# Graph transformer layer followed by a graph attention layer: where the scores stand among TensorE's products, and how one bias row is made

## The chip, the cores and the metric

The kernel runs on one core of one Trainium2 chip, in one launch. The metric is the device time of that core in microseconds (us). Everything is float32.

## The reference, cut to what matters

x has 128 batches of 128 tokens with 512 features, adj 128 matrices of 128 x 128. Two layers follow one another, each on a layer norm with a relu:

```python
h = relu(layernorm(x))
q, k, v = h @ Wq.T + bq, h @ Wk.T + bk, h @ Wv.T + bv     # 8 heads of 64
scores = (q @ k.T) / 8 * (adj + adj)                      # per head
ctx = softmax(scores) @ v
x = x + ctx @ Wo.T + bo

h = relu(layernorm(x))
Wh = h @ W
e = leaky_relu(Wh @ a[:512] + (Wh @ a[512:]).T)
att = softmax(where(adj > 0.5, e, -9e15), axis=1)
x = x + elu(att @ Wh)
```

## The kernel before, in words

**Tiling.** A step p handles a pair of batches, called a and b (64 steps). A group g is two steps, four batches. In layer 0 the projections of a whole group are made by a scheme of 26 block products in place of 32 (a fast matrix multiplication in blocks): for each of the 26 terms n, `Qn` (`product_qk`, L297) makes the products for q and k, and `Vn` (`product_v`, L306) that for v. Their left or right factors are blocks of the normalised input (`hA`) or sums of such blocks, made by `Tn` on GpSimd (`make_form`, L282, tile `tf`, 8 buffers). Four chains of running sums in PSUM, for q/k and for v, are read by `An` (`take_qk`) and `Bn` (`take_v`).

**A step of layer 0.** `sca` and `scb` (`scores`, L367) make the scores of batch a and of batch b. Each head has 64 features, so one product contracts over 64 partitions only, and two heads stand in the two halves of the array's rows. The scores of one batch fill two PSUM tiles of a bank each. `ata0/1` and `atb0/1` (`weigh`, L374, VectorE) read them; maxima, exponentials, sums and division follow (`mx`, `ex`, `rc`, `nm`), then a transposition in blocks with a trip through DRAM (`fl`, `bl`, `pl`). `pca` and `pcb` (`context`, L435) make the contexts: 64 output columns per head, two heads in the two halves of the array's columns. `pe` (ScalarE) and `cs0` to `cs3` (VectorE) read them. `o0` to `o6` (`product_rows`, L346) are the seven products of the output projection, added to x by `od...`.

**A step of layer 1.** `st`, `pw`, `nm`, `h2`, `d..` make the norm and the two dot products, `wm` to `sw` the attention weights, `g0`, `g1` (`gather1`, L528) gather, `ge` and `gs0` to `gs3` read, `w0` to `w6` (`product_rows` again) are seven products, read by `zc...` (ScalarE, L542) and `wd...` (VectorE).

**Banks.** All PSUM tiles come from one pool of 8 banks (`ps1`). A `row_a` tile has two halves: products 0, 2, 4, 5 run up a sum in the first half, which is read after each of them, and product 1 ("b") has the second half. Products 3 and 6 have a tile of their own, `row_c`.

**Order.** Nothing is scheduled by the compiler: three lists, `HEAD`, `ORDER` and `TAIL`, written out in the kernel, give the order of all steps. `ORDER` is run 27 times, for the groups 2 to 28, once for each; a word such as `scb:0` names a step and its distance in p. Each engine takes its own instructions in this order. In `ORDER` before, the steps of TensorE around scores and contexts stand thus: `V23 pca:1 pcb:1 scb:0 w2`, `o6 sca:-1 V5`, `V12 pca:0 pcb:0 scb:-1 Q17` and `o3 sca:-2 Q24`.

**The bias row.** The weights of attention sum to 1, so the bias of v can be added behind the output projection: c = Wo bv + bo - 1. It is made once, in `HEAD`: `ccp` (`product_c`, L578) multiplies 16 blocks of Wo with columns of bv, one output column each; `ccd` (L584) adds bo and -1; `ccs` (`turn_column`, L600) turns the four columns into rows on all partitions with four transposes; `cch` (L603) copies them to `c_sb`. `sh` (GpSimd, L270) adds `c_sb` to x.

Of the kernel before, what the change touches and what calls it, by code (L numbers as in the profile page):

```python
# [13 lines left out]
P = 128  # L14
# [3 lines left out]
H = 8  # L18
# [6 lines left out]
def kernel(  # L25
# [113 lines left out]
    bo_sb = column(bo, "bo")  # L139
# [110 lines left out]
    def fetch0(p):  # L250
        r = rows0[p]
        rows0[p] = small.tile([P, 2 * S, 2], F32, name="mr", bufs=2)
        nc.sync.dma_start(
            rows0[p].rearrange("p k s -> p (k s)"), r.rearrange("b p s -> (b p s)").partition_broadcast(P)
        )
# [21 lines left out]
    def make_form(g, k):  # L277

        a, op, b = FORMS[k]
        forms[g, 2 * C + k] = grp.tile([P, 2 * S], F32, name="tf", bufs=8)  # L280
        eng = nc.gpsimd
        eng.tensor_tensor(forms[g, 2 * C + k], form(g, a), form(g, b), OP.add if op == "+" else OP.subtract)  # L282
# [55 lines left out]
    def product_rows(p, left, w, which, n):  # L338

        la, wb, bank = PRODUCTS[n]  # L340
        own = "c" if bank == "c" else "a"
        if n == 0 or n == 3:
            accs[p, which, own] = ps1.tile([P, 2, E // 2], F32, name="row_" + own, tag="ps1")
        acc = row_acc(p, which, bank)
        for c in range(2):
            nc.tensor.matmul(  # L346
                acc, left[:, la, c, :], w[:, wb, c, :], start=n in (0, 3) and c == 0, stop=c == 1, skip_group_check=True
            )

    def row_acc(p, which, bank):  # L350
        return accs[p, which, "c" if bank == "c" else "a"][:, 1 if bank == "b" else 0, :]
# [18 lines left out]
    def weigh(b, k):  # L370
        p, i = divmod(b, 2)
        if b not in ats:
            ats[b] = work.tile([P, H, S], F32, name="at"), *(small.tile([P, H], F32, name=n) for n in ("nmx", "sums", "rs"))
# [196 lines left out]
    ucol, ccol = const.tile([P, 2, C], F32, name="ucol"), const.tile([P, 1, C], F32, name="ccol")  # L570


    def product_c():
        onces["pm"] = pm = ps1.tile([P, C], F32, name="pm", tag="ps1")
        for j in range(C):
            ms = slice(j % 2 * P, (j % 2 + 1) * P)
            for c in range(C):
                nc.tensor.matmul(  # L578
                    pm[:, j : j + 1], wo_sb[:, 2 * (c // 2) + j // 2, c % 2, ms], bv_sb[:, c : c + 1],
                    start=(c == 0), stop=(c == C - 1),  # L580
                )

    def sum_c():
        nc.vector.scalar_tensor_tensor(ccol[:, 0, :], onces["pm"], -1.0, bo_sb, op0=OP.add, op1=OP.add)  # L584
# [17 lines left out]
    def keep_row(name, dst):  # L602
        nc.scalar.copy(dst, onces[name].rearrange("p c k -> p (c k)"))  # L603
# [16 lines left out]
    def listed(text, mark):  # L620
# [3 lines left out]
        lx@0 t0@-5 lx@1 t0@-4 t1@-4 pp@1 L3@0 t1@-5 W0@0 L0@0 hn0@1 tp0@1 ev0@1 hn1@1 tp1@1 W2@0 pp@0 Lo1@0 ev1@1  # L624
        T4@-2 W13@0 hn1@0 tp1@0 ev1@0 hn0@0 tp0@0 T0@-2 Q0@-2 ev0@0 T5@-2 T1@-2 T2@-2 T3@-2 T6@-2 lx@2 t0@-3 W1@0
        la@0 l0@-2 t0@-2 t1@-2 W3@0 Q1@-2 A1@-2 t1@-3 pp@2 L1@0 W4@0 V1@-2 B1@-2 A0@-2 W7@0 W5@0 W8@0 hn1@2 Q3@-2
        A3@-2 Q5@-2 W9@0 hn0@2 V0@-2 B0@-2 W6@0 Q2@-2 A2@-2 tp1@2 ev1@2 W14@0 Q7@-2 L2@0 W16@0 W11@0 W10@0 Q4@-2
        A4@-2 V3@-2 W25@0 V2@-2 B2@-2 W12@0 Q6@-2 W19@0 W15@0 B3@-2 V5@-2 V7@-2 pp@3 hn1@3 V4@-2 B4@-2 tp1@3 W21@0
        V6@-2 hn0@3 tp0@3 ev0@3 tp0@2 T8@-2 W17@0 B7@-2 W18@0 W29@0 T7@-2 T9@-2 T10@-2 T11@-2 T12@-2 A7@-2 V13@-2
        Q13@-2 W20@0 V9@-2 Q9@-2 W26@0 W28@0 B13@-2 B6@-2 A6@-2 Q8@-2 W27@0 W24@0 W33@0 l0@-1 Lo0@0 Lw0@0 la@-1 W31@0  # L630
        W22@0 t0@-1 t1@-1 A13@-2 W23@0 W30@0 V8@-2 V15@-2 A9@-2 Q11@-2 A8@-2 B8@-2 B9@-2 V11@-2 V10@-2 ev1@3 Q15@-2
        A15@-2 B11@-2 A11@-2 Q10@-2 Lu@0 B15@-2 B10@-2 Q17@-2 T0@0 s0@-1 A17@-2 A10@-2 V12@-2 B12@-2 T13@-2 Q14@-2
        V17@-2 B17@-2 A14@-2 T16@-2 T14@-2 V14@-2 Q12@-2 ev0@2 T7@0 T4@0 T1@0 A12@-2 B14@-2 l0@0 t0@0 V19@-2 Q19@-2
        V16@-2 Q16@-2 A19@-2 Q21@-2 B16@-2 Q0@0 B19@-2 V21@-2 V18@-2 A16@-2 Q18@-2 t1@0 A21@-2 sca@0 Lw1@0 cu00@0
        Q20@-2 B21@-2 ata0@0 ata1@0 T15@-2 s0@0 V23@-2 A20@-2 mxa@0 T2@0 V20@-2 V1@0 B1@0 A0@0 T5@0 B20@-2 W32@0
        exa3@0 exa1@0 exa0@0 Q22@-2 A22@-2 Q23@-2 V22@-2 B22@-2 A23@-2 W34@0 rca0@0 Q24@-2 A24@-2 B23@-2 exa2@0
        nma0@0 rca1@0 nma2@0 V24@-2 B24@-2 l0@1 t0@1 t1@1 Wo0@0 V0@0 nma1@0 nma3@0 fla@0 B0@0 scb@0 T8@0 Q25@-2
        V25@-2 T3@0 V3@0 B3@0 atb0@0 Q1@0 A1@0 V2@0 Q2@0 B2@0 V4@0 B4@0 atb1@0 T9@0 T6@0 T15@0 B25@-2 Q3@0 V6@0 A2@0
        Q4@0 T10@0 A3@0 Q5@0 Q7@0 V5@0 V7@0 B6@0 V8@0 mxb@0 exb3@0 A25@-2 Wo1@0 cu01@0 sca@1 scb@1 l0@2 t1@2 exb1@0
        exb0@0 rcb0@0 exb2@0 A7@0 rcb1@0 f0@1 B8@0 V10@0 t0@2 Ww0@0 lT@1 hd0@1 nmb1@0 A4@0 Q6@0 Q9@0 hd1@1 B7@0 V9@0  # L640
        nmb2@0 nmb0@0 nmb3@0 flb@0 ata1@1 ata0@1 A6@0 Q8@0 Ww1@0 A9@0 B9@0 V11@0 Q11@0 s0@1 T11@0 T12@0 mxa@1 Q13@0
        A13@0 B10@0 A8@0 Q10@0 V13@0 Q15@0 B13@0 V15@0 bla@0 pla@0 pca@0 exa2@1 A10@0 A11@0 B15@0 exa3@1 rca1@1 Q12@0
        exa1@1 exa0@1 A15@0 Q17@0 f0@0 lT@0 T13@0 T0@2 V14@0 rca0@1 B11@0 Ww3@0 nma3@1 A12@0 Wo3@0 V12@0 B12@0 nma0@1
        nma1@1 nma2@1 fla@1 A17@0 atb1@1 Q14@0 T14@0 l0@3 blb@0 plb@0 la@1 atb0@1 B14@0 V17@0 B17@0 ccp@0 ccd@0 A14@0
        mxb@1 pcb@0 T16@0 pea@0 peb@0 ccs@0 Q19@0 o0@0 t0@3 Wo2@0 A19@0 V19@0 B19@0 exb0@1 Q16@0 exb2@1 V16@0 o1@0
        exb3@1 cs2@0 cs0@0 A16@0 V0@2 V21@0 cs1@0 hd0@0 hd1@0 cch@0 Q18@0 Q20@0 exb1@1 rcb0@1 sh@0 B21@0 nmb1@1
        nmb0@1 Q21@0 A20@0 Q22@0 T7@2 f0@2 B16@0 V18@0 rcb1@1 cs3@0 od0@0 o2@0 bla@1 A21@0 sca@2 A22@0 sh@1 Q23@0
        V20@0 V23@0 Q24@0 nmb3@1 nmb2@1 pla@1 flb@1 ata1@2 ata0@2 T1@2 od2@0 o4@0 t1@3 mxa@2 exa1@2 o3@0 T3@2 od1@0
        od4@0 sup0@0 B20@0 V22@0 exa0@2 o5@0 A23@0 B22@0 V24@0 rca0@2 A24@0 Q25@0 od4c@0 o6@0 exa3@2 nma1@2 od5@0
        B24@0 blb@1 plb@1 V25@0 st0@0 exa2@2 rca1@2 od6@0 B23@0 lt@0 nma0@2 sua0@0 T2@2 T4@2 sh@2 T8@2 nma3@2 nma2@2  # L650
        s0@2 T5@2 Q1@2 A1@2 Q0@2 A25@0 st1@0 A0@2 pw@0 cu10@0 nm@0 B25@0 cu11@0 pca@1 lT@2 hd0@2 lT@3 h20@0 d00@0
        pcb@1 peb@1 h21@0 d10@0 scb@2 cs0@1 fla@2 Q3@2 pea@1 V1@2 B1@2 px@0 f0@3 atb0@2 pd@0 bla@2 atb1@2 Q2@2 cs2@1
        B0@2 V2@2 V3@2 B2@2 V4@2 o0@1 o1@1 A2@2 Q4@2 B3@2 V5@2 V7@2 A3@2 mxb@2 B4@2 od0@1 cs1@1 hd1@2 o2@1 od2@1 B7@2
        la@2 hd0@3 hd1@3 sup1@0 o3@1 A4@2 exb1@2 exb3@2 V9@2 exb0@2 sua1@0 B9@2 exb2@2 d11@0 o4@1 od4@1 Q5@2 Q6@2
        A6@2 cs3@1 o5@1 od4c@1 o6@1 pv@0 d01@0 wm@0 od1@1 rcb1@2 od5@1 rcb0@2 pr@0 m1@0 od6@1 st0@1 st1@1 s0@3 e1@0
        sw@0 nmb2@2 V6@2 sca@3 Q7@2 Q8@2 l0@4 g1@0 g0@0 t1@4 A7@2 Q9@2 nmb3@2 nmb1@2 B6@2 nmb0@2 flb@2 pla@2 blb@2
        pw@1 nm@1 T9@2 T6@2 ata1@3 ata0@3 ge1@0 A8@2 Q10@2 ge0@0 T10@2 T11@2 T12@2 A9@2 V11@2 Q11@2 B11@2 gs0@0 A10@2
        mxa@3 h20@1 V8@2 w0@0 h21@1 B8@2 V10@2 Q13@2 gs2@0 gs1@0 A11@2 exa2@3 exa1@3 T16@2 T13@2 V13@2 w1@0 Q12@2
        T14@2 A13@2 Q15@2 B13@2 plb@2 V15@2 lt@1 d11@1 exa0@3 zc0@0 Ww2@0 d00@1 exa3@3 w2@0 zc2@0 A15@2 Q17@2 gs3@0
# [275 lines left out]
```

## Time and profile before

| what | value |
|---|---|
| median of 3 runs | 2343.03 us (2341.63 to 2343.36) |
| the profiled execution, its own time | 2340.49 us |
| its span, first to last instruction | 2338.7 us |
| mean granted TensorE clock | 0.996 |
| busy: PE, DVE, ACT, POOL | 99%, 90%, 63%, 41% |
| a period of ORDER, from the starts of its first contexts | 71.3 us |
| DVE busy, ACT busy in 71.33 us (1198.62 to 1269.95) | 65.64 us, 45.73 us |

A line of the timeline gives the start, the time, the engine and line, the operation, what it writes and reads, the shapes and how many records are merged. One float32 product leaves two MATMUL records. The records of PE overlap (the end of each is modelled), so the pace of TensorE is read from starts: the start of the next group less the start of this one.

### The profile page before, as it was taken

How to read it: one execution, taken by the hardware profiler on the slowest of the kernel's cores; microseconds unless marked ns; L12 is line 12 of the kernel's file. 1: busy time of each engine (PE TensorE's matmuls, PEld its weight loads, DVE VectorE, ACT ScalarE, POOL GpSimd, SP SyncE). 2: the span in 40 equal slices, each digit the busy share in tenths (PEclk: the TensorE clock that was granted, in tenths of full speed). 3: DMA queues.
4: the chain of work that ended last, by engine and by line, in shares of the span. 5: the costliest groups of instructions: out<-in, count | busy, mean ns of one | idle time of the engine just before them, and what ended most of it. 6: DMA issues, size and time to landing. Idle time of an engine off the chain costs nothing.

```text
span 2338.7 us, 45871 instructions
## 1 busy us (share of the span) xinstructions
PE 2311.8 (99%) x15464; PEld 2048.8 (88%) x15464; DVE 2106.2 (90%) x4620; ACT 1470.5 (63%) x4943; POOL 963.5 (41%) x1112
## 2 busy tenths in 40 slices
PE   8999999999999999999999999999999999999998
PEld 7888888888888888888888888888888888889886
DVE  8898889899898999898999999988998999888897
ACT  2666666666666666666666666666666666666764
POOL 4534433444434444334444334443344443444211
PEclk9999999999999999999999999999999999999999
DMA  5434444444454454444453544444444545434333
GB/s 167 127 109 136 143 145 129 127 140 148 126 152 122 132 147 145 140 129 127 140 153 121 149 125 131 147 147 138 131 125 140 154 126 152 121 121 138 117 114 95
DMA packets 267859, 314.37 MB, mean 134 GB/s; under 512 B 24168, under 2 KB 194152, under 8 KB 267624
## 3 DMA queue, kind: packets, MB, share of 16 engines
q1 hardware_dynamic: 263592, 311.31, 44.1%
q8 instruction: 123, 2.02, 0.4%
q14 instruction: 112, 0.92, 0.2%
q0 software_dynamic: 1920, 0.13, 0.1%
q10 hardware_dynamic: 2112, 0.01, 0.1%
HBM read 210.51 MB, written 100.85 MB: 133 GB/s over the span
## 4 chain that ended last, share of the span: by engine, by line
PE 95%; DVE 2%; DMA 1%; POOL 1%; ACT 1%; issue 1%; SPq 0%; POOLq 0%; DVEq 0%; ACTq 0%
PE acc_q L297 31%; PE row_a L346 23%; PE acc_v L306 16%; PE row_c L346 9%; PE sc L367 6%; PE pc L435 5%; PE pg L528 5%; DMA x<-in_x 0%; DMA mr<-rows 0%; DVE st L205 0%; DVE x L449 0%; DVE junk L472 0%; POOL hA L263 0%; PE pm L578 0%; POOL mv L213 0%
## 5 line engine op out<-in xcount | busy, mean ns | idle before, releaser
L297 PE MATMUL acc_q<-tf,w 128*128 128x256 f32 x2176 | 554.3, 384 | 3.6 <-DVE w L170 2.7
L386 ACT ACTIVATE at<-at,nmx 128x128 f32<-128x128 f32 x1024 | 398.4, 395 | 197.4 <-DVE nmx L381 197.4
L282 POOL TENSOR_TENSOR tf<-hA,tf 128x256 f32<-128x256 f32 x288 | 254.7, 889 | 645.6 <-PE acc_v L306 616.5
L297 PEld LDWEIGHTS acc_q<-tf,w 128*128 128x128 f32 x2176 | 392.0, 191 | 59.4 <-issue 5.3
L395 ACT ACTIVATE at<-at,rs 128x128 f32<-128x128 f32 x1024 | 336.8, 394 | 117.5 <-DVE rs L390 117.5
L323 DVE TENSOR_TENSOR qk<-qk,acc_q 128x512 f32<-128x512 f32 x512 | 341.4, 677 | 69.4 <-PE acc_q L297 69.0
L306 PEld LDWEIGHTS acc_v<-w,tf 128*128 128x128 f32 x2176 | 318.9, 191 | 27.0 <-PE row_a L346 0.9
L346 PE MATMUL row_a<-wo,cxT 128*128 128x256 f32 x1280 | 329.9, 381 | 6.0 <-DVE x L449 3.0
L346 PE MATMUL row_a<-w,gT 128*128 128x256 f32 x1280 | 331.1, 385 | 4.7 <-ACT z L542 3.4
L306 PE MATMUL acc_v<-w,tf 128*128 128x128 f32 x2176 | 325.8, 275 | 0.7 <-DVE at L374 0.6
L297 PE MATMUL acc_q<-hA,w 128*128 128x256 f32 x1152 | 298.4, 382 | 0.9 <-ACT qk L321 0.9
L346 PEld LDWEIGHTS row_a<-w,gT 128*128 128x128 f32 x1280 | 230.2, 190 | 41.1 <-ACT z L542 10.7
L346 PEld LDWEIGHTS row_a<-wo,cxT 128*128 128x128 f32 x1280 | 232.7, 190 | 37.2 <-DVE x L449 5.5
L297 PEld LDWEIGHTS acc_q<-hA,w 128*128 128x128 f32 x1152 | 211.0, 190 | 35.6 <-DVE qk L323 8.9
L542 ACT COPY z<-row_a 128x256 f32<-128x256 f32 x256 | 93.9, 367 | 223.2 <-PE row_a L346 222.5
L336 DVE TENSOR_TENSOR v<-v,acc_v 128x256 f32<-128x256 f32 x512 | 205.8, 407 | 27.6 <-PE acc_v L306 27.3
L263 POOL TENSOR_TENSOR hA<-hA,mr 128x512 f32<-128x512 f32 x120 | 164.6, 1392 | 134.7 <-DMA mr<-rows 130.2
L270 POOL TENSOR_TENSOR x<-x,c 128x512 f32<-128x512 f32 x128 | 160.9, 1277 | 139.7 <-ACT qk L321 65.9
L472 DVE SCALAR_TENSOR_TENSOR junk<-h,u 128x512 f32<-128x512 f32 x256 | 195.7, 764 | 7.2 <-ACT h L465 1.6
L386 ACT ACTIVATION_READ_ACCUMULATOR at<-at,nmx 128x1 f32 x1024 | 197.5, 193 | 0.0
L321 ACT ACTIVATE qk<-acc_q,bq 128x256 f32<-128x256 f32 x256 | 120.8, 472 | 121.2 <-PE acc_q L297 121.0
L282 POOL TENSOR_TENSOR tf<-hA 128x256 f32<-128x256 f32 x128 | 121.4, 949 | 152.7 <-DVE hA L265 88.1
(94 smaller groups left out, 4153.5 us busy)
## 6 DMA issues: line engine op xcount, KB each, us to landing
blocks<-tr SPq DMA_DIRECT2D x128, 512.0 KB, 3.0
aT<-blocks SPq DMA_DIRECT2D x512, 128.0 KB, 3.8
x<-in_x SPq DMA_DIRECT2D x123, 512.0 KB, 3.7
out<-x SPq DMA_DIRECT2D x63, 512.0 KB, 3.1
hA<-in_xT SPq DMA_DIRECT2D x120, 256.0 KB, 5.7
mr<-rows SPq DMA_DIRECT2D x60, 256.0 KB, 4.9
adj<-in_adj SPq DMA_DIRECT2D x64, 128.0 KB, 4.7
adjT<-in_adjT SPq DMA_DIRECT2D x64, 128.0 KB, 3.9
```

The lines of the kernel that those rows point to most:

```text
L263: nc.gpsimd.tensor_tensor(h[:, c : c + 2], h[:, c : c + 2], row[:, c : c + 2], OP.subtract)
L270: nc.gpsimd.tensor_tensor(xs[p][:, i, :], xs[p][:, i, :], c_sb, OP.add)
L282: eng.tensor_tensor(forms[g, 2 * C + k], form(g, a), form(g, b), OP.add if op == "+" else OP.subtract)
L297: nc.tensor.matmul(acc[:, i, :], w_sb[:, slot, i, :], form(g, f), start=fresh and i == 0, stop=True, skip_group_check=True)
L306: nc.tensor.matmul(acc[:, i, :], form(g, f)[:, i * P : (i + 1) * P], w_sb[:, slot, 2, :], start=fresh and i == 0, stop=True, skip_group_ch ...
L323: nc.vector.tensor_tensor(d, d, acc, OP.add if sign > 0 else OP.subtract)
L336: nc.vector.tensor_tensor(d, d, acc, OP.add if sign > 0 else OP.subtract)
L346: nc.tensor.matmul(acc, left[:, la, c, :], w[:, wb, c, :], start=n in (0, 3) and c == 0, stop=c == 1, skip_group_check=True)
L367: nc.tensor.matmul(sc[s][:, j, :], qT[r, j, cols], kT[r, j, cols], start=True, stop=True)
L386: nc.scalar.activation(at[:, j, :], at[:, j, :], AF.Exp, bias=nmx[:, j : j + 1], accum_out=sums[:, j : j + 1])
L395: nc.scalar.activation(at[:, j, :], at[:, j, :], AF.Copy, scale=rs[:, j : j + 1])
L472: nc.vector.scalar_tensor_tensor(junk, h2[:, i, :], 1.0, u_sb[:, k, :], op0=OP.mult, op1=OP.mult, accum_out=ws[:, i, 1:2] if k else src_sb ...
```

## The change

It has four parts.

1. The lists are written anew. In `ORDER`, the steps of TensorE around scores and contexts now stand as `V23 pca:1 pcb:1 sca:0 scb:0 w0` and `Q15 pca:0 sca:-1 scb:-1 pcb:0 Q17`. `ORDER` still runs 27 times. `HEAD` has 730 words in place of 789, `TAIL` 1051 in place of 993, as some steps moved from one list to another.
2. Both batches of a step now have their scores at once, so `at` has 2 buffers in place of 1. Room for it comes from `tf`, 6 buffers in place of 8, and `mr` (the norm's numbers, spread over partitions), 1 in place of 2.
3. The bias row: `product_c` has as stationary operand a column of bv broadcast to 128 columns, and moves 256 columns of Wo, so its 8 products give the row on all partitions directly. bo is loaded with a broadcast into `c_sb` (`Lc`), and `ccd` adds in place. `ccs`, `cch` and the column bo are gone.
4. For the last two steps (`alone`), product 1 has a bank of its own, named "b", in place of the second half of `row_a`; the first product that is issued into a bank starts it.

```diff
@@
-        rows0[p] = small.tile([P, 2 * S, 2], F32, name="mr", bufs=2)
+        rows0[p] = small.tile([P, 2 * S, 2], F32, name="mr", bufs=1)
...
-        forms[g, 2 * C + k] = grp.tile([P, 2 * S], F32, name="tf", bufs=8)
+        forms[g, 2 * C + k] = grp.tile([P, 2 * S], F32, name="tf", bufs=6)
...
     def product_rows(p, left, w, which, n):
         la, wb, bank = PRODUCTS[n]
-        own = "c" if bank == "c" else "a"
-        if n == 0 or n == 3:
+        own = bank if bank == "c" or alone(p) else "a"
+        if n == 0 or n == 3 or n == 1 and alone(p):
             accs[p, which, own] = ps1.tile([P, 2, E // 2], F32, name="row_" + own, tag="ps1")
+            begun.discard((p, which, own))
         acc = row_acc(p, which, bank)
         for c in range(2):
+            first = (p, which, own) not in begun
+            begun.add((p, which, own))
             nc.tensor.matmul(
-                acc, left[:, la, c, :], w[:, wb, c, :], start=n in (0, 3) and c == 0, stop=c == 1, skip_group_check=True
+                acc, left[:, la, c, :], w[:, wb, c, :], start=first, stop=c == 1, skip_group_check=True
             )
+    def alone(p):
+        return p >= B // 2 - 2
...
-            ats[b] = work.tile([P, H, S], F32, name="at"), *(small.tile([P, H], F32, name=n) for n in ("nmx", "sums", "rs"))
+            ats[b] = work.tile([P, H, S], F32, name="at", bufs=2), *(small.tile([P, H], F32, name=n) for n in ("nmx", "sums", "rs"))
...
     def product_c():
-        onces["pm"] = pm = ps1.tile([P, C], F32, name="pm", tag="ps1")
-        for j in range(C):
-            ms = slice(j % 2 * P, (j % 2 + 1) * P)
+        onces["pm"] = pm = ps1.tile([P, E], F32, name="pm", tag="ps1")
+        for f in range(2):
             for c in range(C):
                 nc.tensor.matmul(
-                    pm[:, j : j + 1], wo_sb[:, 2 * (c // 2) + j // 2, c % 2, ms], bv_sb[:, c : c + 1],
-                    start=(c == 0), stop=(c == C - 1),
+                    pm[:, f * 2 * P : (f + 1) * 2 * P], bv_sb[:, c : c + 1].to_broadcast([P, P]),
+                    wo_sb[:, 2 * (c // 2) + f, c % 2, :], start=(c == 0), stop=(c == C - 1),
                 )
     def sum_c():
-        nc.vector.scalar_tensor_tensor(ccol[:, 0, :], onces["pm"], -1.0, bo_sb, op0=OP.add, op1=OP.add)
+        nc.vector.scalar_tensor_tensor(c_sb, onces["pm"], -1.0, c_sb, op0=OP.add, op1=OP.add)
...
     ORDER = """
-        Q25:2 A25:2 gs1:3 pw:2 nm:2 h21:2 B21:2 V25:2 w0:3 w1:3 Q1:0 gs3:3 V23:2 plb:1 B25:2 zc0:3 pca:1 A23:2 nma3:0
-        d10:2 h20:2 d11:2 pea:1 d00:2 rca0:0 pcb:1 peb:1 lT:0 A1:0 lx:1 f0:0 scb:0 s0:0 nma1:0 w2:3 px:2 pd:2 cs0:1
-        t0:-1 B23:2 cs1:1 o0:1 nma0:0 cs2:1 Q3:0 o1:1 zc2:3 w4:3 fla:0 zc4:3 lT:-1 V1:0 bla:0 w5:3 sh:1 pv:2 od0:1
...
-        nma3:-1 d10:1 d01:1 V12:0 B12:0 lt:1 pca:0 pea:0 B15:0 plb:0 pcb:0 peb:0 fla:-1 so:3 scb:-1 atb1:-1 atb0:-1
...
-        B20:0 blb:-1 o3:0 sca:-2 ata1:-2 T16:0 Q24:0 V22:0 ata0:-2 Q23:0 o1:0 ez:2 od4c:0 e1:1 sw:1 V21:0 mxa:-2
...
+        A23:2 g0:3 ge0:3 Q25:2 A25:2 ge1:3 gs0:3 V24:2 B24:2 T8:0 V23:2 B23:2 gs1:3 so:4 gs2:3 gs3:3 pca:1 pcb:1
+        sca:0 scb:0 pea:1 peb:1 pw:2 nm:2 h20:2 h21:2 ata0:0 w0:3 zc0:3 ata1:0 V25:2 cs0:1 mxa:0 exa1:0 exa0:0 d10:2
+        d00:2 atb1:0 px:2 rca0:0 atb0:0 w2:3 T1:0 Q2:0 zc2:3 T3:0 T2:0 f0:0 Q1:0 V1:0 exa2:0 T7:0 t0:-2 nma0:0 w4:3
...
+        V5:0 la:-2 lt:0 blb:0 od6:1 B2:0 V4:0 pr:2 m1:2 B4:0 A6:0 e1:2 V7:0 s0:-2 T6:0 T9:0 B7:0 od5:1 Q7:0 A7:0
+        hd0:-1 Q8:0 st0:1 Q9:0 sw:2 A9:0 V6:0 pla:0 V9:0 B9:0 g1:2 st1:1 hd1:-1 zc5:3 fa:3 T10:0 V11:0 g0:2 B6:0 V8:0
...
+        gs2:2 pw:1 nm:1 h21:1 h20:1 V12:0 A10:0 gs1:2 B12:0 Q12:0 A12:0 Q15:0 A15:0 pca:0 sca:-1 scb:-1 pcb:0 ata1:-1
...
-                "ccs": lambda: turn_column(ccol[:, 0, :], "c"), "cch": lambda: keep_row("c", c_sb),
+                "Lc": lambda: load_rows(c_sb[:, None, :], bo),
```

## The prediction

> **What bounds the kernel now.** I read the page's busy shares and slices first, then the chain that ended last.
>
> ```profile
> PE 2311.8 (99%) x15464; PEld 2048.8 (88%) x15464; DVE 2106.2 (90%) x4620; ACT 1470.5 (63%) x4943; POOL 963.5 (41%) x1112
> PE   8999999999999999999999999999999999999998
> PE 95%; DVE 2%; DMA 1%; POOL 1%; ACT 1%; issue 1%; SPq 0%; POOLq 0%; DVEq 0%; ACTq 0%
> ```
>
> TensorE is busy from end to end and carries 95% of the chain; only the first and last slice have holes. So time can come only from TensorE's own stream (fewer or cheaper products, cheaper passages between them) and from those two ends. Next I read the timeline of PE within one period of ORDER, start to start.
>
> ```profile
> 1209.41 1.03 PE L346 MATMUL row_c<-wo,cxT 128*128 128x256 f32 x4
> 1210.37 1.16 PE L367 MATMUL sc<-qk 64*128 64x128 f32 x16
> 1211.46 0.71 PE L306 MATMUL acc_v<-w,hA 128*128 128x128 f32 x4
> 1212.01 1.14 PE L528 MATMUL pg<-w,h 128*128 128x128 f32 x8
> ...
> 1228.02 0.61 PE L306 MATMUL acc_v<-w,hA 128*128 128x128 f32 x4
> 1228.56 1.97 PE L435 MATMUL pc<-aT,v 128*64 128x128 f32 x32
> 1230.46 1.16 PE L367 MATMUL sc<-qk 64*128 64x128 f32 x16
> 1231.55 2.06 PE L297 MATMUL acc_q<-tf,w 128*128 128x256 f32 x8
> 1233.44 0.61 PE L306 MATMUL acc_v<-w,tf 128*128 128x128 f32 x4
> ```
>
> The undisturbed pace, read off many such rows: 0.865 us for four records of 256 columns, 0.445 for four of 128, and 0.889 for the 16 records of scores or contexts of one batch (half of 16 x 0.111, as two heads run beside each other). Against this pace the rows have excess. row_c takes 0.96, 0.10 over. The scores take 1.09, 0.20 over. The group behind them takes 0.55 in place of 0.445, 0.10 over. So scores that stand alone cost 0.40 us beyond their work. Behind two contexts: 0.10 into the contexts, 1.90 for 1.778 (0.12), 0.20 out of the scores, 0.10 after: 0.52. (The 1.89 for eight records holds 0.055 more; that I count as a wait.) Where scores follow scores, and where a context follows scores:
>
> ```profile
> 72.51 2.06 PE L367 MATMUL sc<-qk 64*128 64x128 f32 x32
> 74.49 0.71 PE L306 MATMUL acc_v<-w,tf 128*128 128x128 f32 x4
> 75.04 1.03 PE L297 MATMUL acc_q<-tf,w 128*128 128x256 f32 x4
> ...
> 2252.62 1.16 PE L367 MATMUL sc<-qk 64*128 64x128 f32 x16
> 2253.71 1.09 PE L435 MATMUL pc<-aT,v 128*64 128x128 f32 x16
> 2254.74 1.13 PE L346 MATMUL row_a<-w,gT 128*128 128x256 f32 x4
> ```
>
> Two scores take 1.98 for 1.778: again only 0.20. The second is free of excess. A context behind scores takes 1.03 for 0.889, 0.14 to leave it.
>
> The waits that reach TensorE in the steady part are small, two per period:
>
> ```profile
> PEld row_a L346 <- ACT z L542: 10.7, 31, 2.4
> PEld acc_q L297 <- DVE qk L323: 9.8, 31, 0.4
> ```
>
> **What the Trainium skill says.** "TensorEngine Tiling (Array Packing)", Key Properties: a change of tiling mode, not of the tile alone, drains TensorE. The trace agrees: 0.40 us per isolated visit, none between two scores. "TensorE: Matmul & The Clock Gate", What's actually happening: an array that is too little busy is clocked at half rate. The trace shows it in the head, behind the products of one column (below). "PSUM — Partial Sum Buffer", PSUM bank collisions: two engines must not access one bank at once, whatever the columns. That bears on the last part; the trace shows no such pair apart from other waits.
>
> **Part 1, scores together.** Before, a period of ORDER has four visits to the tiled modes: two alone (0.40 each) and two behind contexts (0.52 each), 1.84 us. After, it has two. Contexts, contexts, scores, scores: 0.10 + 0.12 + 0.20 + 0.10 = 0.52. Context, scores, scores, context: 0.10 + 0.12 + 0.20 + 0.14 + 0.10 = 0.66. Sum 1.18, so 0.66 less; with unrounded starts 0.65. Times 27 periods: **17.6 us**, all on the path. HEAD: counting runs in the lists, before 5 scores alone (2.00), 2 single contexts (0.33 each), scores twice (0.41), and 2 mixed runs (0.52 each), 4.1; after 2 alone, scores twice, contexts twice (0.33), and 2 mixed runs of four (0.53), 2.6: **1.5 us**. TAIL: 15 runs before, 6.5 us; 13 after, 5.6: **0.9 us**. The work itself is unchanged: 832 Q, 832 V, 896 row products, 128 each of scores, contexts, gathers.
>
> **Part 2, buffers and new order.** The second `at` adds no instruction. It lets `atb` run while batch a is still in softmax. Six forms in place of eight: a T waits for the last product that reads its slot, on GpSimd, which is 41% busy and already idles on such waits; behind a late T stand the other T, `sh`, `hd0` and `pw` in its queue, and TensorE's Q or V for it. By the list, T1, T3, T2 are asked for right before Q2 and Q1, but the slots they take are free after V21, V24 and V23, over 5 us earlier: nothing. One `mr`: the fetch waits for hd1 of the step before on SP; from f0:-1 to hd0:-1 there are 7 us of TensorE work for a 4.9 us landing: nothing, and 0.7 us per glitch if not. Behind it in SP's queue stand the loads of adj and adjT, with several us each to spare. Of the two waits of before, a row product that follows its predecessor with one V between recurs (w0, V25, w2; before w4, V1, w5, 0.28 us), and Q7, Q8, Q9 is like Q11, w0, Q12 (0.18). I take the waits as unchanged, 0.5 us per period. Bounds: all gone, 14 us better; doubled, 14 us worse.
>
> **Part 3, the bias row.**
>
> ```profile
> 88.25 4.62 PE L578 MATMUL pm<-bv,wo 128*128 128x1 f32 x32
> 94.70 1.12 PE L600 MATMUL pu<-ident,ccol 128*128 128x128 f32 x4
> 95.61 1.91 PE L297 MATMUL acc_q<-tf,w 128*128 128x256 f32 x4
> 97.32 1.12 PE L346 MATMUL row_a<-wo,cxT 128*128 128x256 f32 x4
> ...
> 94.60:97.30 2.70, 2.70 (x10) 2.26 (x9) 1.55 (x4) 2.48 (x12) 0.00 (x0) 0.50 0.50 140
> ```
>
> From 88.25 to 92.80 the 32 records take 4.55 us. After, 8 products of 256 columns are 16 records of 0.216, 3.46: 1.09 less. The broadcast weight load is no bound: the loads of the broadcast ucol took 137 ns against 191 for others. The transposes (0.91) go. The granted clock was 0.50 there, so acc_q took 1.71 in place of 0.865, and pc at 92.80 1.90 for some 1.03; with a fully streaming product this may vanish, 0.85 + 0.87. From 2.0 to 3.7 us; I take **3.0**. `ccd` grows from 0.16 to about 0.68 us on VectorE (the row of `at`, same size), `cch` (0.57 on ScalarE) goes; neither is on the path. `Lc` is 256 KB on SP, some 0.5 us of issue like the other row load, in front of x0 loads; hidden by TensorE's work, 0.5 us if not.
>
> **Part 4, own bank.** In the last two steps, `zc0` could start behind w0 rather than w1. Stalls of TensorE on ACT z there are 0.46 and 0.51 us long, and the copy at 2327.85 also stood behind an exponential. So 0 to 2 us; I take **1.0**.
>
> **Sum.** 17.6 + 1.5 + 0.9 + 3.0 + 1.0 = 24.0. The profiled execution (2340.5, span 2338.7 and 1.8 around it) becomes 2316.5; it lies 2.5 under the median of the runs, so the median goes from 2343.0 to 2319.0. VectorE then has some 65 of 70.6 us per period: 92%, no bound yet.
>
> **Rivals.** *Slower: banks.* A visit holds up to six of eight banks, two contexts and four scores. Before sca:0, VectorE must clear A25, B24, B23 and gs0 to gs3: 0.6 + 6 x 0.33 = 2.6 us within 2.9 us from the end of Q25; w0 behind scb needs the first bank back from `ata`, 0.68 us, within 1.2. For it: margins of 0.3 us and VectorE at 92%. Against: in the old order equally tight pairs held. If VectorE is one `at` late (0.7 us) at each of 54 visits: 37.8 - 24.0 = 13.8, **2357**. It turns the sign from 0.44 us per visit. *Partly eaten*: new waits of 0.45 us per period (a late T or copy) take 12: **2331**. *No change*: waits of 0.9 us per period: **2343**. *Better*: the new list also removes the old waits: 14 more, **2305**. *The drain is not saved*, as it belongs to each scores group: the row at 72.51 speaks against it; then about 2339.
>
> **How the numbers follow.** Likeliest, 2308 to 2330: 0.66. Partly eaten, 2330 to 2338: 0.12. No change: 0.06. Slower: 0.09. Better, under 2308: 0.07. The range 2306 to 2338 leaves out 0.05 below and 0.15 above. This kernel's measurement tells 0.2%, 4.7 us, from no change; by it faster 0.85, same 0.06, slower 0.09.
>
> **What would show it.** In the profile after: a period near 70.6 us; sc x32 groups of some 1.98 us with 0.1 before and after; no isolated sc x16 in ORDER; pm of some 3.5 us with the clock at 1.0; PE still at 99%. It is wrong if PE idles behind sc until DVE `at` or before row_a or sc for a bank, if acc_q waits for POOL tf, or if the excess around sc x32 is 0.8.

## The result, and the profile after

The changed kernel takes 2328.1 us in the median of four runs (2323.18 to 2329.05), the kernel before 2342.33 beside it: a ratio of 0.9937, 95% interval 0.9919 to 0.9954, or 14.2 us less. Forecast were 24.0 us less (2319.0). Sign and range hold; the gain is three fifths of the forecast. The profiled execution of after is its fastest, 2323.18 us with a span of 2321.4; the other runs lie near 2328. The page's lines on TensorE and the chain:

```profile
PE 2291.4 (99%) x15444; PEld 2037.5 (88%) x15444; DVE 2099.9 (90%) x4620; ACT 1460.3 (63%) x4942; POOL 972.8 (42%) x1112
PE   8999999999999999999999999999999999999998
PE 92%; DVE 4%; DMA 1%; ACT 1%; issue 1%; POOL 1%; SPq 0%; POOLq 0%; DVEq 0%; ACTq 0%
```

TensorE has 20 instructions fewer and 20.4 us less busy time, and still fills the span. The share of DVE in the chain doubled, from 2% to 4%: TensorE's stream is handed over to other engines somewhat more often than before. The timeline of PE shows both visits to scores and contexts in a pass of ORDER, and the start of the next pass:

```profile
1209.71 1.03 PE L296 MATMUL acc_q<-tf,w 128*128 128x256 f32 x4
1210.66 1.09 PE L441 MATMUL pc<-aT,v 128*64 128x128 f32 x16
1211.69 2.06 PE L373 MATMUL sc<-qk 64*128 64x128 f32 x32
1213.67 1.09 PE L441 MATMUL pc<-aT,v 128*64 128x128 f32 x16
1214.70 1.99 PE L296 MATMUL acc_q<-tf,w 128*128 128x256 f32 x8
1216.53 0.81 PE L348 MATMUL row_a<-w,gT 128*128 128x256 f32 x3
...
1244.49 1.97 PE L441 MATMUL pc<-aT,v 128*64 128x128 f32 x32
1246.38 2.06 PE L373 MATMUL sc<-qk 64*128 64x128 f32 x32
1248.37 1.13 PE L348 MATMUL row_a<-w,gT 128*128 128x256 f32 x4
1249.34 0.61 PE L305 MATMUL acc_v<-w,hA 128*128 128x128 f32 x4
1250.02 1.13 PE L348 MATMUL row_a<-w,gT 128*128 128x256 f32 x4
...
1281.62 1.09 PE L441 MATMUL pc<-aT,v 128*64 128x128 f32 x16
```

From start to start, the 32 scores take 1.98 us (1211.69 to 1213.67) and 1.99, as two scores together did at 72.51 of the kernel before. With 0.10 into it, 0.13, 0.20 and 0.14 inside and 0.10 behind, the first visit costs 0.67 us beyond its work; the second, 0.10 + 0.11 + 0.21 + 0.10, costs 0.53. That is 1.20 for a forecast of 1.18. But the period is 1281.62 - 1210.66 = 70.96 us for 71.31 before: 0.36 less, not 0.65. The rows behind the second visit show where the rest is. acc_v at 1249.34 has four records of 128 columns, 0.445 us of work, and the next product starts 0.68 later. The time that the loads of weights waited for others:

```profile
PEld row_a L348 <- DVE x L455: 10.0, 31, 0.9
...
PEld row_a L348 <- ACT z L548: 8.5, 30, 0.9
PEld acc_q L296 <- ACT qk L320: 8.4, 29, 0.3
...
PEld acc_q L296 <- DVE qk L322: 5.1, 29, 0.5
```

The columns are the total in us, the number of times and the longest. Four sorts of wait occur in nearly every pass where the prediction showed two. The last of them, Q9 for `A7`, is over before Q8 has ended and costs TensorE nothing; a fourth that does reach TensorE, Q10 for `A8`, shows only as a late start in the timeline of PE. With the 0.10 us that the product behind each takes more, they are, from start to start: w2 for `zc0` (z), 0.33; o4 for `od2` (x), 0.15; Q8 for `A6` (qk L320), 0.16; Q10 for `A8`, 0.16. The sum is 0.80 us per pass. Before it was 0.52: the 0.28 and 0.18 of the prediction, and the 0.055 that it counted as a wait.

The bias row in HEAD, in the timeline and in two windows of time (length; busy time of PE, PEld, DVE, ACT and POOL, each with its count; then the granted clock, the DMA share and GB/s):

```profile
79.67 0.71 PE L305 MATMUL acc_v<-w,tf 128*128 128x128 f32 x4 [1.78 <-POOL tf L281]
80.22 3.62 PE L583 MATMUL pm<-wo,bv 128*128 128x256 f32 x16
83.67 0.61 PE L305 MATMUL acc_v<-w,tf 128*128 128x128 f32 x4
```

```profile
80.00:84.00 4.00, 4.00 (x23) 3.59 (x22) 2.77 (x7) 0.00 (x0) 1.15 (x2) 1.00 0.96 280
84.00:100.00 16.00, 16.00 (x116) 14.50 (x115) 14.66 (x33) 11.07 (x43) 10.67 (x11) 1.00 0.33 71
```

The 16 records of pm take 3.45 us (80.22 to 83.67; forecast 3.46), and in this profile the clock is 1.00 during and behind them, where it had been 0.50. The transposes of this row are gone. The row above pm is a new stall of 1.78 us for a form. In the timeline of GpSimd six sums of forms stand one behind the other there, from 75.60 on; the one that ends just ahead of acc_v runs from 78.89 to 79.62. It was late by its own queue, ahead of which GpSimd had stood idle for 2.77 us until the first `mr` landed (69.40).

### The profile page after: what moved, and what is told of

It is laid out like the page before. It is cut to its first block, busy times and chain, and to the rows that moved or that the text cites. A ratio compares the mean times of both kernels' runs of the same rounds, so it can differ in the third digit from the quotient of the medians.

```text
span 2321.4 us, 45352 instructions
## 1 busy us (share of the span) xinstructions
PE 2291.4 (99%) x15444; PEld 2037.5 (88%) x15444; DVE 2099.9 (90%) x4620; ACT 1460.3 (63%) x4942; POOL 972.8 (42%) x1112
## 4 chain that ended last, share of the span: by engine, by line
PE 92%; DVE 4%; DMA 1%; ACT 1%; issue 1%; POOL 1%; SPq 0%; POOLq 0%; DVEq 0%; ACTq 0%
PE acc_q L296 30%; PE row_a L348 24%; PE acc_v L305 14%; PE row_c L348 9%; PE pc L441 5%; PE sc L373 5%; PE pg L534 5%; DVE st L204 1%; DVE w L169 1%; DVE qk L322 1%; ACT z L548 1%; DMA aT<-blocks 0%; DMA w<-in_wT 0%; DVE junk L478 0%; DVE x L455 0%
## 5 line engine op out<-in xcount | busy, mean ns | idle before, releaser
L281 POOL TENSOR_TENSOR tf<-hA,tf 128x256 f32<-128x256 f32 x288 | 225.0, 786 | 660.7 <-PE acc_v L305 642.4
L305 PEld LDWEIGHTS acc_v<-w,tf 128*128 128x128 f32 x2176 | 312.4, 191 | 24.7 <-POOL tf L281 2.1
L401 ACT ACTIVATE at<-at,rs 128x128 f32<-128x128 f32 x1024 | 329.1, 396 | 1.2 <-DVE rs L396 1.2
L348 PE MATMUL row_a<-wo,cxT 128*128 128x256 f32 x1272 | 320.9, 382 | 0.8 <-DVE x L455 0.5
L380 DVE SCALAR_TENSOR_TENSOR at<-sc,adj 128x512 f32<-128x512 f32 x256 | 166.1, 681 | 44.3 <-PE sc L373 44.2
L281 POOL TENSOR_TENSOR tf<-hA 128x256 f32<-128x256 f32 x128 | 93.4, 741 | 257.8 <-PE acc_v L305 194.0
L320 ACT ACTIVATE qk<-acc_q,bq 128x256 f32<-128x256 f32 x256 | 120.1, 469 | 113.7 <-PE acc_q L296 113.6
L269 POOL TENSOR_TENSOR x<-x,c 128x512 f32<-128x512 f32 x128 | 174.9, 1386 | 22.5 <-DMA x<-in_x 9.5
```

The source lines that it names most:

```text
L269: nc.gpsimd.tensor_tensor(xs[p][:, i, :], xs[p][:, i, :], c_sb, OP.add)
L305: nc.tensor.matmul(acc[:, i, :], form(g, f)[:, i * P : (i + 1) * P], w_sb[:, slot, 2, :], start=fresh and i == 0, stop=True, skip_group_ch ...
L320: nc.scalar.activation(d[:, i, :], acc[:, i, :], AF.Identity, bias=bias[:, j : j + 1], scale=float(sign))
L348: nc.tensor.matmul(acc, left[:, la, c, :], w[:, wb, c, :], start=first, stop=c == 1, skip_group_check=True)
L380: nc.vector.scalar_tensor_tensor(ats[b][0][:, k * C : (k + 1) * C, :], scs[b][k], QSCALE, adjs[p][:, i : i + 1, :].to_broadcast([P, C, S]) ...
L401: nc.scalar.activation(at[:, j, :], at[:, j, :], AF.Copy, scale=rs[:, j : j + 1])
```

## The experiments

Theory A: TensorE is the bound, the passages cost what the prediction says, and the shortfall is the new waits and nothing else; then each wait that a neighbour's move takes away comes back in full. Theory B: VectorE, busy for 90% of the span, has become the hidden bound of a period; then moves on TensorE bring back little, and the waits reappear elsewhere. A period is always taken from a `pc` start to the same one in the next pass.

**The changed kernel again.**

> The changed kernel once more, beside the others. Theory A (the visits are paid by the drain, and the new list waits 0.27 us more per period): a period of 70.95 us again, median some 15 to 19 us below the kernel before. Theory B (the median of 14 us is what the change is worth, and a profile that lies 17 us lower is an exception): median 13 to 15 us below, with a period above 71.0 us or more time in the two ends.

2326.78 us, ratio 0.9929 (0.9917 to 0.9942), the period 70.95 in every pass. Its profiled execution took 2328.92, 5.7 more than the one above, with the same period. Most of this is the granted clock. In three stretches of 3.4 us it was 0.50 here, where it was 1.00 in the other profile. The first falls on the products of the bias row:

```profile
80.02 0.71 PE L305 MATMUL acc_v<-w,tf 128*128 128x128 f32 x4 [2.01 <-POOL tf L281]
80.56 5.30 PE L583 MATMUL pm<-wo,bv 128*128 128x256 f32 x16
85.71 0.61 PE L305 MATMUL acc_v<-w,tf 128*128 128x128 f32 x4
```

```profile
81.06:84.47 3.41, 3.41 (x10) 2.67 (x9) 1.06 (x3) 0.00 (x0) 0.51 (x1) 0.50 0.90 269
```

pm takes 5.15 us in place of 3.45, and the steady part begins 2.0 us later (first contexts at 182.18 for 180.23). The other two lie in TAIL, from 2265.59 and from 2303.13; there, from the last lone context but two to the last product, it takes 54.0 us for 50.9. All three begin at the end of a wait of TensorE or within 1.1 us behind it (waits of 2.01, 1.75 and 1.35 us). Such a wait did not always bring the clock down. The eleven profiles of this list and its variants below all have the wait for a form ahead of pm. In seven of them, with waits of 1.65 to 3.04 us, the clock then falls and pm takes 4.46 to 5.71 us; in four, with waits of 1.47 to 1.92, it stays and pm takes 3.45 or 3.46. So one kernel varies by 0.2% in its two ends, and effects there of 1 or 2 us can't be told from medians alone.

**Each batch of scores alone again.** `scb` leaves `sca`, in both visits.

```diff
-  d00:2 atb1:0 px:2 rca0:0 atb0:0 w2:3 T1:0
+  d00:2 px:2 rca0:0 w2:3 scb:0 atb1:0 atb0:0 T1:0
-  pca:0 sca:-1 scb:-1 pcb:0 ... atb1:-1 mxa:-1 Q17:0 T13:0
+  pca:0 sca:-1 pcb:0 ... mxa:-1 Q17:0 scb:-1 atb1:-1 T13:0
```

> ORDER of the changed kernel with the scores of the second batch taken out of the pair: scb:0 behind w2:3, scb:-1 behind Q17:0, each alone among full products. Theory A (each isolated visit costs 0.40 us): the period goes from 70.95 to 71.74 us, +0.79, and the time up by 21 us. Theory B (the cost belongs to each group of scores wherever it stands, and the gain came from the new list otherwise): the period stays within 0.1 us.

2349.23 us, ratio 1.0021 (1.0011 to 1.0031): 22.4 us over the changed kernel. The period is 71.74, 0.79 longer, twice the 0.40 of the prediction. PE in its timeline:

```profile
1225.99 1.16 PE L373 MATMUL sc<-qk 64*128 64x128 f32 x16
1227.08 1.09 PE L441 MATMUL pc<-aT,v 128*64 128x128 f32 x16
1228.10 1.13 PE L296 MATMUL acc_q<-tf,w 128*128 128x256 f32 x4
1229.16 1.16 PE L373 MATMUL sc<-qk 64*128 64x128 f32 x16
1230.26 1.13 PE L296 MATMUL acc_q<-tf,w 128*128 128x256 f32 x4
1231.22 1.89 PE L348 MATMUL row_a<-w,gT 128*128 128x256 f32 x8
```

Between the contexts the 16 scores leave with 0.20 over their work (1.09 for 0.889), and so do the 16 that stand alone at 1229.16 (1.10). The acc_q rows around these hold 0.10 each for entry and 0.10 for the product behind. The passage belongs to the visit, not to the batch: theory A, and this part of the prediction, hold.

**Four neighbours changed places.**

```diff
-  w2:3 T1:0 Q2:0        o4:1 o3:1 w6:3     Q9:0 sw:2 A9:0 V6:0    Q10:0 plb:0 Q13:0
+  T1:0 Q2:0 w2:3        w6:3 o4:1 o3:1     V6:0 Q9:0 sw:2 A9:0    plb:0 Q13:0 Q10:0
```

> ORDER of the changed kernel with four products of TensorE moved by one place, so that a read of PSUM has longer before the next product onto it: w2:3 behind Q2:0, Q10:0 behind Q13:0, Q9:0 behind V6:0, o4:1 and o3:1 behind w6:3. Theory A (these four reads hold TensorE some 0.79 us per period): the period goes to some 70.2 us, 19 to 21 us less. Theory B (VectorE at 92% is a hidden bound and each wait returns at another place): the period stays above 70.7 us.

2333.9 us, ratio 0.9958 (0.9945 to 0.997), slower than the changed kernel. The period is 71.21. The waits of w2 and o4 are gone, 0.48 less. But Q13, drawn forward, now stands ahead of the form that it needs:

```profile
1213.44 0.61 PE L305 MATMUL acc_v<-w,tf 128*128 128x128 f32 x4
1214.53 1.78 PE L296 MATMUL acc_q<-tf,w 128*128 128x256 f32 x7 [0.48 <-POOL tf L281]
```

From 1213.44 to 1214.53 are 1.09 us for 0.445 of work: 0.65, and 0.10 behind, in each pass, where Q10 had lost 0.16. With 0.19 at the product behind V9, which also came earlier, that makes -0.48 + 0.59 + 0.19 = 0.30 for the measured 0.26. Nor did moving Q9 help, since it is Q8 that waits: I had moved the wrong product. The freed time didn't come back as waits for VectorE, which speaks against theory B, but A's number wasn't reached, so the test is taken up again below.

**Both contexts first in the second visit.**

```diff
-  pca:0 sca:-1 scb:-1 pcb:0 ata1:-1
+  pca:0 pcb:0 sca:-1 scb:-1 ata1:-1
```

> ORDER of the changed kernel with pcb:0 ahead of sca:-1, so that the second visit, too, runs context, context, scores, scores. Theory A (a passage from scores back to a context costs 0.14 us more): the period falls by 0.14 us to 70.81, 4 us in all. Theory B (the list has the second context last because its transposed weights or the banks for the scores come no earlier): TensorE waits there and the period is 70.95 us or more.

2384.55 us, ratio 1.0167 (1.0152 to 1.0181): 57.8 us worse for a visit that is itself cheaper (0.52 for 0.67). The period is 73.14, 2.19 longer, and most of that is one wait, by the list for PE (total, number, longest):

```profile
PE acc_q L296 <- DVE qk L322: 46.9, 26, 1.8
```

The timeline of DVE ahead of that copy:

```profile
1259.45 0.67 DVE L478 SCALAR_TENSOR_TENSOR junk<-h,u 128x512 f32<-128x512 f32 x1
1260.05 0.08 DVE L478 DVE_READ_ACCUMULATOR junk<-h,u 128x1 f32 x1
1260.16 3.02 DVE L478 SCALAR_TENSOR_TENSOR junk<-h,u 128x512 f32<-128x512 f32 x1
```

and of GpSimd in that time:

```profile
1260.53 1.42 POOL L281 TENSOR_TENSOR tf<-hA 128x256 f32<-128x256 f32 x2
1261.90 0.72 POOL L281 TENSOR_TENSOR tf<-hA,tf 128x256 f32<-128x256 f32 x1
```

One dot product takes 0.67 us, and the next of the same shape 3.02, when GpSimd's three sums run. It ends at 1263.18, 0.56 us behind the end of the last sum (1262.62). In the second profile of the changed kernel it takes 0.69, beside GpSimd's step on `mv` (2 columns), and there it is that step which is longer, 1.15 us for 0.71. Measured from the start of GpSimd's `sh` ahead of both (1255.51 here, 1223.82 there), the dot came 1.1 us later, and GpSimd, not held up on `mv`, began its sums 0.9 us earlier: so they met. Of the 1.1 us an earlier dot had lost 0.86, as it now fell beside `sh`:

```profile
1255.75 1.57 DVE L478 SCALAR_TENSOR_TENSOR junk<-h,u 128x512 f32<-128x512 f32 x1
```

In the changed kernel that dot took 0.71. Neither theory had this reason. "SBUF — State Buffer", Who interferes with whom, of the Trainium skill says that a VectorE instruction with two inputs in SBUF contends with a GpSimd instruction that reads SBUF, since its second input comes through a read interface that the two share; the rows of the dot and of the sums agree. The same section says that the order of issue decides who is held up. The starts in the timeline don't show that here: the dot began 0.37 us ahead of the first sum and still ended behind the last. The starts on GpSimd are rough, and what decides it stays open.

**The same with the dot later**, just ahead of `wm`, behind GpSimd's sums. In the timeline it now starts 4.4 us behind the place that it had (1243.11, where VectorE would have come to it at 1238.7).

```diff
-  pca:0 sca:-1 scb:-1 pcb:0 ... d11:1 d01:1 nma1:-1 ... flb:-1 wm:1
+  pca:0 pcb:0 sca:-1 scb:-1 ... d11:1 nma1:-1 ... flb:-1 d01:1 wm:1
```

> Both contexts ahead of the scores in the second visit (pca, pcb, sca, scb), as in the run that took 57.8 us more; and VectorE's dot d01 of that half period is moved from behind d11 to just ahead of wm, some 2.5 us later, behind GpSimd's three sums. If the loss of that run came from VectorE's dot and GpSimd's sums running at once, the 1.98 us wait for qk goes, the mean of the dot's line falls from 1092 to about 780 ns, and the period is 70.95 - 0.13 = 70.8 us: ratio 0.991 to 0.993. If the loss came from the order of the products itself (scores and probabilities later, banks free later), the period stays near 73 us and the ratio near 1.017.

2343.04 us, ratio 0.999 (0.9976 to 1.0004): 41.5 us of the loss are gone, but not all. Of 26 periods 14 are the forecast 70.8 us (70.80 to 71.01); the others are up to 2.5 us longer. In this kernel the mean of the dot's line is 848 ns (1092 in the run before, 782 in the changed kernel), and its mask step `wm` waits:

```profile
L508 DVE SCALAR_TENSOR_TENSOR w<-adjT,w x62: 384/412/427, 133.1 to 2286.7; 128x256 f32<-128x256 f32 x62
...
  DMA w<-row: 17.9, 12
```

Twelve of its 62 executions wait for a row that comes by DMA, 17.9 us in all (two, 1.0 us, in the second profile of the changed kernel), and behind `wm` in VectorE's queue stand the z and qk that TensorE then waits for. The median from issue to landing of that row is 5.1 us for 3.9:

```profile
w<-row SPq DMA_DIRECT2D x62, 128.0 KB, 5.1
```

The dot itself takes 0.65 us at its new place. With it out of the way VectorE's transposes end earlier, and the 512 KB writes of `blocks` start 0.9 us sooner behind the row's issue (2.9 us for 3.8). That these delay the row is likely, but it wasn't tried alone.

**The bias row alone**, in the kernel before: `product_c`, `sum_c` and `Lc` as in the change; `ccs` and `cch` gone.

```diff
-  "ccs": lambda: turn_column(ccol[:, 0, :], "c"), "cch": lambda: keep_row("c", c_sb),
+  "Lc": lambda: load_rows(c_sb[:, None, :], bo),
```

> The kernel before with the bias row of the change alone (8 products of 256 columns with a broadcast stationary operand, bo by a broadcast load, the four transposes and the copy left out). Theory A: pm takes 3.5 in place of 4.55 us, the granted clock no longer falls to 0.50 behind it, 2.0 to 3.7 us less in all, 3.0 likeliest. Theory B (TensorE waits in the head for other engines anyway): the head ends at the same time and the total is unchanged within 1 us.

2340.25 us, ratio 0.998 (0.9967 to 0.9994) to the kernel before, 4.7 us by the ratio with an interval from 1.4 to 7.7. The trace tells more. In the kernel before, a pair of contexts early in the steady part reads:

```profile
189.51 1.97 PE L435 MATMUL pc<-aT,v 128*64 128x128 f32 x32
```

and in this one:

```profile
186.84 1.97 PE L434 MATMUL pc<-aT,v 128*64 128x128 f32 x32
```

2.7 us earlier, within the forecast 2.0 to 3.7 us. One pass later it is 4.3 us, as the first pass of the kernel before holds 1.6 us of stalls more (73.34 us for 71.74); whether that belongs to the bias row, one profile of each does not tell. The clock stands at 1.00 from 84 to 100 us here, and in the kernel before at 0.50 from 90.67 to 97.49:

```profile
84.00:100.00 16.00, 15.58 (x107) 13.59 (x106) 15.36 (x30) 9.15 (x40) 7.52 (x7) 1.00 0.54 150
```

```profile
90.67:97.49 6.82, 6.82 (x36) 6.11 (x37) 4.14 (x9) 2.67 (x12) 0.00 (x0) 0.50 0.58 176
```

No stall of TensorE stands ahead of it there, which leaves the products of one column as what lowered it. That rests on one profile of each.

**The bank of its own taken back**, in the changed kernel; o0 and o1 of the last step change places so that the first still starts the bank.

```diff
-        return p >= B // 2 - 2
+        return False
```

> The changed kernel with product 1 of the last two steps in the second half of row_a again, as before (o0 ahead of o1 in the last step, as the first product into the bank must be product 0). Theory A: the copy behind w0 has to wait for w1, 0 to 2 us more, 1.0 likeliest. Theory B (ScalarE's copy stands behind an exponential anyway): no difference beyond 0.3 us in the tail.

2331.81 us, ratio 0.994 (0.9926 to 0.9953), for 0.9929 (0.9917 to 0.9942) with the bank: the intervals overlap. In the profiles, from the last lone context but two to the start of the last product, it takes 54.9 us with the shared bank, for 50.9 and 54.0 in the two profiles with the own one (the 54.0 with the lower clock told of above, which neither of the others has there). PE has a wait that is otherwise 0.7 us or less:

```profile
PE row_a L348 <- DVE x L455: 3.6, 2, 2.1
```

The 2.1 us are o1 in the last step but one: it goes on in the bank from which `od0` is still to read the first half. The bank is worth 4.0 us between the two profiles of equal clock, 0.9 against the other, and 0.0011 of 2343, 2.6 us, by the ratios, which alone don't tell it from nothing. That holds for the new TAIL, which was made with the bank.

**Two of the neighbours only.** w2 behind Q2, and w6 ahead of o4 and o3.

```diff
-  atb0:0 w2:3 T1:0 Q2:0 zc2:3        nma2:0 o4:1 o3:1 w6:3 od4:1
+  atb0:0 T1:0 Q2:0 w2:3 zc2:3        nma2:0 w6:3 o4:1 o3:1 od4:1
```

> Two neighbours on TensorE change places in the list of the changed kernel: w2 goes behind Q2, and w6 goes ahead of o4 and o3. Theory A (TensorE is the bound, and each wait between two products is pure loss): the waits for zc0 (0.33 us with its drain) and for od2 (0.15 us) go and nothing comes in their place, so the period falls from 70.95 to 70.47 us and the time by 27 x 0.48 = 13.0 us, to a ratio of about 0.987 to the kernel before. Theory B (VectorE, busy for 90% of the span, is the hidden bound of the period): the period stays within 0.15 us of 70.95, the ratio at about 0.993, and new waits for VectorE stand in the trace.

2313.64 us, ratio 0.9875 (0.9862 to 0.9887), with 0.987 forecast by theory A. The period is 70.46 in every pass. PE behind the second visit, and around o4:

```profile
1239.78 2.06 PE L373 MATMUL sc<-qk 64*128 64x128 f32 x32
1241.77 1.13 PE L348 MATMUL row_a<-w,gT 128*128 128x256 f32 x4
1242.73 0.61 PE L305 MATMUL acc_v<-w,hA 128*128 128x128 f32 x4
1243.18 1.03 PE L296 MATMUL acc_q<-tf,w 128*128 128x256 f32 x4
1244.04 1.03 PE L348 MATMUL row_a<-w,gT 128*128 128x256 f32 x4
1244.91 1.03 PE L296 MATMUL acc_q<-tf,w 128*128 128x256 f32 x4
```

acc_v now takes 0.45 (1242.73 to 1243.18) in place of 0.68, and the rows behind it run at 0.865. The work is the same, only Q2 covers the copy that w2 needs. Theory A is right for these two waits, and B falls: VectorE had the room to follow.

**All four waits by moves on ScalarE too.** The two swaps stay, and copies on ScalarE change places. Q8 writes on into the bank that `A6` reads, and Q10 into that of `A8`. Both copies had their data before and stood behind others in ScalarE's queue.

```diff
-  m1:2 B4:0 A6:0     A9:0 V6:0           ez:3 gs0:2 B8:0     fb:3 A8:0 Q10:0
+  m1:2 A6:0 B4:0     A9:0 A8:0 V6:0      gs0:2 B8:0 ez:3     fb:3 Q10:0
```

> The two swaps of w2 and w6, and on ScalarE alone: A6 ahead of B4, A8 directly behind A9, and ez behind B8, so that A6 and A8 have read their banks before Q8 and Q10 write on into them. Theory A: all four steady waits of the changed kernel (0.33, 0.15, 0.16 and 0.16 us) go, the period falls to 70.15 us and the time by 27 x 0.80 = 21.6 us, to a ratio of about 0.984. Theory B: the period stays within 0.3 us of 70.95, with waits for VectorE or ScalarE at other products; the ratio stays above 0.990.

2324.66 us, ratio 0.9923 (0.991 to 0.9936): worse than two swaps alone. The period is 70.78. A8 takes 0.85 us of ScalarE ahead of B9, and V11 waits for B9, in each of 27 passes:

```profile
PE acc_v L305 <- ACT v L333: 6.5, 27, 0.2
```

Counted from start to start it costs 0.42 us, and 0.08 behind.

**Mended**: A8 behind B6 in place of behind A9, the rest as there.

```diff
-  A9:0 A8:0 V6:0 ... B6:0 V8:0
+  A9:0 V6:0 ... B6:0 A8:0 V8:0
```

> As the run with four moves, but A8 stands behind B6 on ScalarE in place of ahead of B9: in that run A8 held back B9 by 0.85 us, V11 waited for it (0.42 us with its drain), and the period was 70.78 in place of 70.15 us. Theory A: with that wait gone none of the four steady waits is left and none is new: period 70.15 us, 27 x 0.80 = 21.6 us below the changed kernel and 27 x 0.31 = 8.4 us below the two swaps alone, a ratio of 0.983 to 0.985. Theory B (ScalarE and VectorE have no slack left for it): a new wait of 0.2 us or more in each period, and a ratio no lower than that of the two swaps, 0.9875.

2311.33 us, ratio 0.9859 (0.9843 to 0.9876): the fastest of all, though its interval overlaps that of the two swaps. The period is 70.30, not 70.15. V11's wait and Q10's are gone. Q8's moved on by one product. Its loads of weights:

```profile
1192.89 0.84 PEld L296 LDWEIGHTS acc_q<-tf,w 128*128 128x128 f32 x4
1194.04 0.73 PEld L296 LDWEIGHTS acc_q<-hA,w 128*128 128x128 f32 x4 [0.32 <-DVE qk L322]
```

Q8 (1192.89) is no longer late, so Q9 catches up with `A7`, which can't begin before Q7 has ended; TensorE loses 0.18 there in place of 0.16. So of 0.80 us 0.65 came back, and the last part needs other work between Q7 and Q9.

**Everything together**: the first four moves on both engines, both contexts first, the dot later.

```diff
-  atb0:0 w2:3 T1:0 Q2:0 zc2:3        nma2:0 o4:1 o3:1 w6:3 od4:1
+  atb0:0 T1:0 Q2:0 w2:3 zc2:3        nma2:0 w6:3 o4:1 o3:1 od4:1
-  m1:2 B4:0 A6:0     A9:0 V6:0           ez:3 gs0:2 B8:0     fb:3 A8:0 Q10:0
+  m1:2 A6:0 B4:0     A9:0 A8:0 V6:0      gs0:2 B8:0 ez:3     fb:3 Q10:0
-  pca:0 sca:-1 scb:-1 pcb:0 ... d11:1 d01:1 nma1:-1 ... flb:-1 wm:1
+  pca:0 pcb:0 sca:-1 scb:-1 ... d11:1 nma1:-1 ... flb:-1 d01:1 wm:1
```

> All moves of the two other runs together: w2, w6, A6, A8, ez, both contexts first in the second visit, and the dot d01 later. Theory A: the gains add up, 0.80 + 0.13 us per period, to a period of 70.0 us and a ratio of about 0.982. Theory B: no better than the changed kernel, 0.990 or more. If the moved dot meets other work of GpSimd, VectorE falls behind as before, and the ratio goes over 1.

2337.57 us, ratio 0.9973 (0.9966 to 0.9981). The best passes take 70.63 us, others up to 72.9, with V11's wait and the late row of the two runs in one. It tells nothing new, except that the gains do not add up once VectorE's order is disturbed.

## Why the prediction was right in direction and too high

- **What bounds the kernel**: right. TensorE is busy for 99% of the span before and after, and every gain and loss of a period is found in rows of its timeline.
- **Part 1, the passages**: right. Forecast 0.65 us less per pass; measured 1.84 for 1.20 per pass, 0.64. The run with the scores apart gives it back, 0.79 with its two lone batches at 0.40 each. It was worth 27 x 0.64 = 17.3 us.
- **Part 2, "I take the waits as unchanged, 0.5 us per period"**: this step failed. The waits cost 0.80, so 0.28 to 0.29 of the 0.64 went back in each pass: 27 x 0.29 = 7.8 us of the 9.8 us by which the gain missed. The pair w0, V25, w2 was foreseen at 0.28 and costs 0.33; the second, Q7, Q8, Q9, was foreseen at 0.18 and costs 0.16. Two were not foreseen, 0.15 and 0.16: o4 behind w1 for `od2`, and Q10 for `A8`. On ScalarE `A8` (1205.68) stood behind `B8`, which itself waited for V8 until 1205.40; the 1.06 us exponential `ez` ahead of `B8` had ended at 1205.16. The working looked only for pairs like the two of before, although the whole list was new. The two swaps removed 0.48 and gained 13 us (0.9929 to 0.9875), which is what shows that these waits, and no hidden bound, took it. The "partly eaten" rival put this at 0.45 per period with "a late T or copy"; copies it was, and 0.28.
- **Part 2, six forms and one `mr`**: in ORDER no wait for a form or for `mr` reaches TensorE in the profile. In HEAD one for a form does, of 1.47 to 3.04 us in the eleven profiles, from a full queue on GpSimd, and in seven of them the lower clock behind it costs pm 1.0 to 2.3 us more. The prediction looked for late forms in ORDER alone and put this at nothing. That is enough for the 2 us which the waits in the passes leave of the miss, but it wasn't taken away in a run. Whether the list or the fewer slots made the queue wasn't tried apart either; the six sums stand without a gap, so none of them waited for a slot.
- **Part 3, the bias row**: right for the row alone, 2.7 us for 3.0 in the kernel before, with the clock at 1.00. In the changed list pm takes the forecast 3.46 where the clock holds, in four of eleven profiles. One reading did not carry over: the loads of the broadcast column took 190 ns, as others do, and not the 137 read off `ucol`. It cost nothing here.
- **Part 4, own bank**: 4.0 us by the two profiles of equal clock for 1.0 forecast, with 2.6 by the ratios, not clear of noise. Its place was only half seen: the prediction had `zc0` behind w0, and the long stall that the shared bank brings is o1's, for `od0`.
- **The two ends**: by the profiled executions the change gained 17.3 us (2340.49 to 2323.18), 9.7 of it in the 27 passes (0.36 each) and 7.6 elsewhere, for 6.4 forecast in the ends (1.5 + 0.9 + 3.0 + 1.0). Some 3 of the 7.6 are passes of the kernel before that ran over its 71.31 us, the first by 2.0 and a later one by 1.0. That leaves some 4.5, as the medians do: 14.2 - 9.7 = 4.5. With 5 us between two executions of one kernel, most of it from the clock, the 1.5 and 0.9 can't be judged singly.
- **Rivals**: "slower: banks" did not come. No wait for `at` stands in the list for PE of the changed kernel. "The drain is not saved" falls with the run that has the scores apart. VectorE can turn the sign, but by another way: the dot beside GpSimd's sums, in the run with both contexts first.

## What to carry to other kernels

When an order of work is written anew, look in the new list at every product that needs a copy of the one a step or two before, and count what is queued ahead of that copy on its engine; a gain of 0.64 us per pass lost 0.28 in that way, and two neighbours that change places brought more than this back. Where a wait is removed, look for the next product that then catches up with its copy, as Q9 did behind Q8. Before VectorE's work is shifted by a microsecond, see what GpSimd does at the new time. And before two executions are compared, look for stretches of lower clock behind waits of TensorE in each.

## What was not expected of the hardware

One VectorE dot of 512 columns took 3.02 us beside three GpSimd sums in place of 0.67 to 0.69, and ended 0.56 us behind the last of them, while the sums kept their 0.7 us each. Where they met in each pass, the kernel was 57.8 us slower, and moving the dot brought 41.5 of this back.

The granted clock was 0.50 for 6.8 us from 90.67 on, during and behind 32 records of one column, though TensorE was busy throughout by the count. With eight products of 256 columns in their place, in a kernel otherwise the same, it stayed at 1.00. In the changed list, where a wait of TensorE stands just ahead of the same eight products, it fell to 0.50 for 3.4 us or twice that in seven of eleven profiles.
